# First image pair of a fused attention and spectral-convolution layer: transposes on the vector engine and through DRAM, long matmuls along h, inverse transforms with two row groups in two banks

## The chip, the cores and the metric

The kernel runs on one core of a Trainium2 chip. The metric is the device time of one execution in microseconds, the median over runs. A profile is one further execution, recorded instruction by instruction; "span" is the time from its first to its last instruction.

## The reference, cut to what matters

The input x has shape (4, 64, 96, 96): 4 images of 64 channels and 9216 pixels. Two residual layers follow each other.

```python
# layer 0: attention with a sigmoid over all pairs of pixels, channel gate
h = group_norm(x)                                   # 32 groups
Q, K, V = 1x1 convolutions of h (8, 8 and 64 channels), N = 96*96
att = sigmoid(einsum('bcn,bcm->bnm', Q, K))         # 9216 x 9216 per image
y = einsum('bcm,bnm->bcn', V, att) + h
gate = sigmoid(mlp(mean(y)) + mlp(max(y)))          # per channel
x = x + y * gate
# layer 1: spectral convolution
u = rfft2(group_norm(x), norm='ortho')
v = 0 except v[:, :, :16, :16] = einsum('bchw,cohw->bohw', u[:, :, :16, :16], R_pos)
             v[:, :, -16:, :16] = the same with u[:, :, -16:, :16] and R_neg
x = x + irfft2(v, norm='ortho')
```

Only 32 frequencies along h (KH) and 16 along w (KW) are kept, so the Fourier transforms are products with small constant matrices (fw, fh, gh, gw).

## The kernel before, in words

Two images share the 128 partitions (64 channels each): pair 0 and pair 1. Attention goes through 2 x 18 blocks of 512 query pixels. For one block there are 144 tiles of energies (72 chunks of 128 keys, 2 images), each one matmul (L441, on 32 rows, four row groups side by side) into one PSUM bank. ScalarE takes the sigmoid of several banks at once (L452) and writes `at`; TensorE multiplies `at` with the values (L470, 64 columns per image, two column groups side by side) and sums the block up in an accumulator bank.

The tiles of a block are handled in bursts of 6 or 7. `pattern` gives each block one list of burst sizes: `DENSE` (24 bursts of 6), `SPARSE` (21 bursts, nearly all of 7), `HALF` (22 bursts, 10 of 6 and 12 of 7). PSUM has 8 banks: one accumulates, a burst of 7 takes all the others, and a burst of 6 leaves one spare, `bank_a`. The loop at the end of the attention part writes down, for each burst number t: the energies of burst t + 1, then the steps of `mid[t]`, then the value matmuls of about one burst and the sigmoids of burst t + 1, then the steps of `end[t]`. TensorE follows this order.

The steps in `mid` are other work that uses the spare bank: keys, values and queries of later blocks, and, while pair 1 is in attention, the whole of layer 1 for pair 0 (class `Hidden`). `put(t, steps, every)` places each step at the next free t whose following burst has 6 tiles. VectorE and the DMA queue of SyncE (SP) get their instructions in an order that the framework's scheduler chooses within the dependencies; each is worked off strictly in order. A spare bank must be emptied by VectorE before the next burst of 7 can use it.

Layer 1 of pair 0 in steps (blocks 18 to 29):

- `result(s)`, 12 strips of 768 pixels: loads the input strip (`old`), adds the gated attention output in place on VectorE (`combine`, L162), takes statistics (L260); the strip is also stored to DRAM (`x1d`).
- `transposes(r)`, 24 steps: four TensorE transposes of 96 pixels x 128 channels (L270) into the spare bank, copied by VectorE to `xT` (L588).
- `along_w(m)`, 6 steps: four matmuls with fw (L280), each on 32 columns of the array, then a copy, and a way through DRAM (`ad`) that turns the layout into `ah` (rows h).
- statistics in 4 small steps (`st0` to `spread`), then `along_h(i)`, 4 steps: 32 matmuls each with `ah` as the stationary and 64 columns of fh as the moving operand (L307), scaled into `u` by VectorE (L313).
- `mix(q, half)`, 16 steps: products with the weights (L203), which SP streams in.
- `back_h(e, half, b)`, 8 steps: one matmul of 64 rows, 96 columns and 512 moving columns (L326), a copy, a way through DRAM (`zd`) to `z`.
- `back_w(i, x1d)`, 24 steps: two matmuls of 128 rows, 64 columns (one image each), 384 moving columns of gw, side by side (L348), added to the strip from `x1d` by VectorE (L351) and stored to the output.

`gw` is block diagonal: rows of one of its four 32-row blocks meet only the 96 output columns of one image row.

After attention, pair 1 does its own layer 1 in a tail of some 90 us that the change leaves alone (L716 to L831).

Of the kernel before, what the change touches and what calls it, by code (L numbers as in the profile page):

```python
# [40 lines left out]
P = 128  # L41
# [5 lines left out]
KW = 16  # L47
# [8 lines left out]
HALF = [6 if i == 1 or i % 2 == 0 and i < 18 else 7 for i in range(22)]  # L56
SPARSE = [6 if i in (0, 1, 11) else 7 for i in range(21)]
# [24 lines left out]
def tile_kernel(ctx: ExitStack, tc: tile.TileContext, x, cst, late, spec, out):  # L82
# [153 lines left out]
    class Hidden(Layer1):  # L236


        def __init__(self, p, gate, bank, move, work):
            super().__init__(p, gate, bank, move, (nc.sync,) * 3)  # L240
            self.work = work
            self.stats = small.tile([P, 2 * NSTRIP, 6], F32, tag="stats1", name=f"stats1_{p}")
            self.xts, self.ah = {}, None
            self.ad = dram.tile([H, 2 * KW, P], F32, tag=f"ad{p}", name=f"ad_{p}")
            self.zd = dram.tile([H, 2 * KW, 2, C], F32, tag=f"zd{p}", name=f"zd_{p}")
# [8 lines left out]
        def result(self, s):  # L254
            p, cols = self.p, bass.ts(s, STRIP)
            old = self.work.tile([P, STRIP], F32, tag="old", bufs=2, name=f"old_{p}_{s}")
            nc.sync.dma_start(old, xf[bass.ts(p, P), cols])
            self.combine(s, old)
            for i in (2 * s, 2 * s + 1):
                nc.vector.bn_stats(self.stats[:, i, :], xs[p][:, bass.ts(i, STRIP // 2)])  # L260
# [4 lines left out]

        def transposes(self, r):

            pt = self.bank(f"pt_{self.p}_{r}")
            for i in range(4):
                nc.tensor.transpose(pt[:W, bass.ts(i, P)], xs[self.p][:, bass.ts(4 * r + i, W)],  # L270
                                    ident)
            self.xts[r] = self.work.tile([W, NB], F32, tag="xT", bufs=4, name=f"xT_{self.p}_{r}")
            self.move(self.xts[r], pt[:W, :])

        def along_w(self, m):
# [3 lines left out]
            for g in range(4):  # L279
                nc.tensor.matmul(pa[bass.ts(g, 2 * KW), :], named("fw", W), self.xts[4 * m + g],  # L280
                                 start=True, stop=True)
# [12 lines left out]
        def along_h(self, i):  # L294

            b, half = i // 2, i % 2
            ah = self.ah.rearrange("h (s k b c) -> h s k b c", k=KW, b=2, c=C)
            u = self.ut[:, :U].rearrange("q (h k n s b) -> q n k s h b", h=KH, n=SIDE, s=2, b=2)
            if i == 0:
                nc.vector.memset(self.ut[:, U:], 0.0)  # L300
            pu = self.bank(f"pu_{self.p}_{i}")
            fh = named("fh", H)
            for k in range(KW // 2):
                for s in range(2):
                    for part in range(2):
                        first = KH * (2 - s - part)
                        nc.tensor.matmul(pu[bass.ts(part, C), bass.ts(k, 2 * KH)],  # L307
                                         ah[:H, s, half * (KW // 2) + k, b, :],
                                         fh[:, first:first + 2 * KH],
                                         start=(s == 0), stop=(s == 1))  # L310
            v = pu.rearrange("q (n k s h) -> q n k s h", n=2, s=2, h=KH)
            for n in range(2):
                nc.vector.tensor_scalar(u[:, 2 * half + n, :, :, :, b], v[:, n],  # L313
                                        self.rs[:, 0, b:b + 1], None, ALU.mult)
# [5 lines left out]
        def back_h(self, e, half, b):  # L320


            first = e * KW + half * (KW // 2)
            ks, rows = slice(first, first + KW // 2), bass.ts(b, 2 * KH)
            pz = self.bank(f"pz_{self.p}_{b}_{e}_{half}")
            nc.tensor.matmul(pz[:H, :], named("gh")[rows, bass.ts(e, H)],  # L326
                             self.vt[rows, bass.ts(half, KW // 2 * C)], start=True, stop=True)
            zt = self.work.tile([P, NB], F32, tag="ae", bufs=2, name=f"zt_{self.p}_{b}_{first}")
            self.move(zt[:H, :], pz[:H, :])
            nc.sync.dma_start(self.zd[:, ks, b, :],  # L330
                                     zt[:H, :].rearrange("h (k o) -> h k o", o=C))
            if b == 1:
                for j in range(4):
                    nc.sync.dma_start(
                        self.z[32 * j + first:32 * j + first + KW // 2, :, :],
                        self.zd[j::4, ks, :, :].rearrange("h k b o -> k h (b o)"))

        def back_w(self, i, x1d):

            s = i // 2  # L340
            cols = bass.ts(s, STRIP)
            if i % 2 == 0:
                self.old = self.work.tile([P, STRIP], F32, tag="old", bufs=2,
                                          name=f"x1_{self.p}_{s}")
                nc.sync.dma_start(self.old, x1d[:, cols])
            py = self.bank(f"py_{self.p}_{i}")
            for b in range(2):
                nc.tensor.matmul(py[bass.ts(b, C), :4 * W], self.z[:, i, bass.ts(b, C)],  # L348
                                 named("gw"), start=True, stop=True)
            o = self.old[:, bass.ts(i % 2, 4 * W)]  # L350
            nc.vector.tensor_tensor(o, py[:, :4 * W], o, ALU.add)  # L351
            if i % 2:
                nc.sync.dma_start(outf[bass.ts(self.p, P), cols], self.old)


    with tc.tile_pool(name="work", bufs=1) as work, \
# [11 lines left out]
        kT = kvp.tile([P, NCH // 2, P], F32R, tag="kT", name="kT")  # L368

# [64 lines left out]
        def bank_of(t):  # L434
            return 0 if sizes[t] == 7 and block[t] % 2 == 0 else 1
# [94 lines left out]
        pattern = [DENSE] + [SPARSE] * (NBLK - 2) + [DENSE] + [HALF] * 12  # L530
# [14 lines left out]
        def put(t, steps, every=1):  # L545
# [42 lines left out]
        l1 = Hidden(0, gate, bank_a, lambda dst, src: nc.vector.tensor_copy(dst, src), work)  # L588
        x1d = dram.tile([P, N], F32, tag="x1", name="x1d")
        for s in range(NSTRIP):  # L590
            end[first + 7 + 2 * s] += [lambda s=s: later(lambda: (
                l1.result(s), nc.sync.dma_start(x1d[:, bass.ts(s, STRIP)],
                                                xs[0][:, bass.ts(s, STRIP)])))]
        t = put(first + 9, [step for m in range(H // 16) for step in [
            lambda r=r: l1.transposes(r) for r in range(4 * m, 4 * m + 4)] + [
                lambda m=m: l1.along_w(m)]])
# [16 lines left out]
        t = put(t + 2, [lambda i=i: l1.along_h(i) for i in range(4)], 2)  # L613
# [9 lines left out]
        t = put(t + 5, [lambda i=i: l1.back_h(i // 4, i // 2 % 2, i % 2) for i in range(8)])  # L623
        t = put(t + 5, [lambda i=i: l1.back_w(i, x1d) for i in range(H // 4)])
# [293 lines left out]
```

## Time and profile before

| | us |
|---|---|
| runs | 3116.04, 3119.44, 3120.33 (median 3119.44) |
| profiled execution, its own time | 3118.38 |
| its span | 3116.6 |
| TensorE matmul busy | 3072.2 (99%) |
| ScalarE busy | 2424.6 (78%) |
| VectorE busy | 397.0 (13%) |
| mean granted TensorE clock | 0.995 |

1.8 us of the profiled execution lie outside its span. In the profile, a line such as L470 is a line of the kernel before; "x12" counts instructions; a float32 matmul shows as two matmul instructions (two passes). "out<-in" names tiles; "PEld" is TensorE's loading of the stationary operand. The tile `ws` is the memory of pair 0's x after it has been reused as workspace (`u`, weights, `z`), `room` is that of `ah` reused.

### The profile page before, as it was taken

To read this page: it belongs to the slowest core of one execution; us is meant where nothing else is said; L and a number is where in the kernel's file an instruction comes from. 1 tells how busy PE (TensorE), PEld (TensorE's weight loads), DVE (VectorE), ACT (ScalarE), POOL (GpSimd) and SP (SyncE) were. 2 spreads that over 40 slices of the span, in tenths; PEclk is the share of its full clock that TensorE was granted. 3 is DMA by queue.
4 is the path that set the end of the run, shared out by engine and by line. 5 is a ranking of instruction groups with operands and counts; after the bars stand their busy time and mean duration, and the time that the engine had idled before them with its cause. 6 is when DMAs were issued, how large, how long until landed. Compare 5 with 4: busy or idle time off the path is not lost.

```text
span 3116.6 us, 43034 instructions
## 1 busy us (share of the span) xinstructions
PE 3072.2 (99%) x19186; PEld 1147.4 (37%) x19186; DVE 397.0 (13%) x838; ACT 2424.6 (78%) x1585; POOL 24.5 (1%) x49
## 2 busy tenths in 40 slices
PE   6999999999999999999999999999999999999998
PEld 3433333333333333334433333333333333333335
DVE  5300000000000000002331110110101100000015
ACT  3788888888888888886777777777777788888871
POOL 0000000000000000000000000000000010000001
PEclk9999999999999999999999999999999999999998
DMA  3000000000000000000120010131210130000026
GB/s 143 1 1 1 1 1 1 1 1 1 1 1 1 1 1 1 1 1 1 41 88 14 8 36 13 52 125 44 36 34 31 41 120 1 1 1 1 6 74 216
DMA packets 39161, 88.87 MB, mean 29 GB/s; under 512 B 10336, under 2 KB 17248, under 8 KB 38880
## 3 DMA queue, kind: packets, MB, share of 16 engines
q1 hardware_dynamic: 31856, 61.88, 6.4%
q0 software_dynamic: 5344, 19.27, 1.7%
q10 hardware_dynamic: 1776, 4.97, 0.4%
q8 instruction: 150, 2.46, 0.3%
q14 instruction: 35, 0.29, 0.0%
HBM read 62.77 MB, written 23.33 MB: 28 GB/s over the span
## 4 chain that ended last, share of the span: by engine, by line
PE 97%; DVE 1%; DMA 1%; issue 0%; POOL 0%; SPq 0%; ACT 0%; POOLq 0%; DVEq 0%
PE banks L470 74%; PE banks L441 16%; PE banks L409 1%; PE banks L421 1%; PE banks L348 1%; PE banks L398 1%; PE banks L203 1%; DMA x<-in_x_dram 0%; PE py L825 0%; PE banks L270 0%; DVE x L162 0%; DMA old<-in_x_dram 0%; DMA vd<-vm 0%; DVE xt L724 0%; PE banks L326 0%
## 5 line engine op out<-in xcount | busy, mean ns | idle before, releaser
L452 ACT ACTIVATE at<-banks 128x1536 f32<-128x1536 f32 (+1 forms) x1548 | 2404.4, 1597 | 610.6 <-PE banks L441 546.8
L470 PE MATMUL banks<-at,vT 128*64 128x512 f32 (+1 forms) x11728 | 2395.2, 549 | 0.0
L470 PEld LDWEIGHTS banks<-at,vT 128*64 128x64 f32 x11728 | 780.4, 136 | 1348.9 <-issue 1294.1
L441 PE MATMUL banks<-q,kT 32*128 32x512 f32 x5184 | 571.4, 454 | 1.6 <-DVE xT L588 1.6
L441 PEld LDWEIGHTS banks<-q,kT 32*128 32x128 f32 x5184 | 232.9, 182 | 472.3 <-issue 301.5
L475 DVE SCALAR_TENSOR_TENSOR x<-banks,x 128x512 f32<-128x512 f32 x36 | 24.9, 692 | 897.7 <-PE banks L470 897.7
L378 DVE TENSOR_SCALAR full_q<-banks,cs 128x256 f32<-128x256 f32 x36 | 17.4, 484 | 858.8 <-PE banks L421 858.8
L409 PE MATMUL banks<-cs,x 128*64 128x128 f32 x576 | 41.6, 287 | 1.5 <-DVE full_k L378 0.6
L431 DVE CAST q<-q 32x256 fp32r<-32x256 f32 x144 | 40.9, 284 | 3.9
L351 DVE TENSOR_TENSOR x<-banks,x 128x384 f32<-128x384 f32 x24 | 13.4, 558 | 197.0 <-PE banks L348 156.9
L409 PEld LDWEIGHTS banks<-cs,x 128*64 128x64 f32 x576 | 32.3, 141 | 16.2 <-DVE full_k L378 14.6
L588 DVE COPY xT<-banks 96x512 f32<-96x512 f32 x24 | 16.5, 686 | 167.1 <-PE banks L270 167.1
L386 DVE SCALAR_TENSOR_TENSOR q<-high_q,cs,full_q 64x256 fp32r<-64x256 f32 x72 | 34.6, 480 | 2.4
L378 DVE TENSOR_SCALAR full_k<-banks,cs 128x256 f32<-128x256 f32 x36 | 17.4, 484 | 93.2 <-PE banks L398 93.2
L588 DVE COPY ws<-banks 128x512 f32<-128x512 f32 x16 | 11.1, 692 | 141.7 <-PE banks L203 141.7
L412 DVE TENSOR_TENSOR vT<-banks,cs 128x512 f32<-128x512 f32 x36 | 24.8, 689 | 8.4 <-PE banks L409 8.3
L398 PE MATMUL banks<-x,cs 128*64 128x256 f32 x144 | 24.2, 396 | 1.6 <-DVE x L149 1.5
L477 DVE TENSOR_REDUCE maxs<-x 128x1 f32<-128x512 f32 x36 | 24.7, 686 | 1.2
L421 PE MATMUL banks<-x,cs 128*64 128x256 f32 x144 | 23.9, 410 | 0.6 <-DVE full_k L378 0.6
L483 DVE BATCH_NORM_STATS2 stats<-x 128x6 f32<-128x512 f32 x36 | 22.1, 679 | 8.0 <-DMA x<-in_x_dram 8.0
L732 PE MATMUL pa<-xt,lc 128*128 128x256 f32 x72 | 18.9, 422 | 3.6 <-DVE xt L724 2.6
L725 ACT ACTIVATE vT<-x,less 128x768 f32<-128x768 f32 x12 | 11.2, 934 | 12.4 <-DVE x L162 8.4
(117 smaller groups left out, 452.2 us busy)
## 6 DMA issues: line engine op xcount, KB each, us to landing
ws<-in_spec_dram SPq DMA_DIRECT2D x20, 512.0 KB
x<-in_x_dram SPq DMA_DIRECT2D x15, 512.0 KB
out_dram<-x SPq DMA_DIRECT2D x18, 384.0 KB
room<-in_spec_dram SPq DMA_DIRECT2D x12, 512.0 KB
w<-in_spec_dram POOLq DMA_DIRECT2D x10, 512.0 KB, 6.9
old<-in_x_dram SPq DMA_DIRECT2D x12, 384.0 KB
x1d<-x SPq DMA_DIRECT2D x12, 384.0 KB
x<-x1d SPq DMA_DIRECT2D x12, 384.0 KB
```

The costliest lines, as they stand in the source:

```text
L203: self.last = nc.tensor.matmul(pv[bass.ts(g, 32), :].rearrange("q (n k o) -> q n k o", n=SIDE, o=C)[:, :, k, :], self.ut[:, at:at + 32], s ...
L348: nc.tensor.matmul(py[bass.ts(b, C), :4 * W], self.z[:, i, bass.ts(b, C)], named("gw"), start=True, stop=True)
L378: nc.vector.tensor_scalar(u, src, bias, None, ALU.add)
L386: mark[0] = nc.vector.scalar_tensor_tensor(dst, h.bitcast(F32), is_low, u, ALU.mult, ALU.add)
L398: nc.tensor.matmul(pp[cols, :NB // 2], named("wk")[:, cols], src[:, e, :, :], start=True, stop=True)
L409: nc.tensor.matmul(pp[bass.ts(e, P // 2), bass.ts(i, P)], xs[p][:, bass.ts(2 * (4 * s + i) + e, P // 2)], named("wv"), start=True, stop=True)
L421: nc.tensor.matmul(pq[rows, :half], named("wq")[:, rows], xs[p][:, n * NB + e * half:n * NB + (e + 1) * half], start=True, stop=True)
L431: nc.vector.tensor_copy(q[to:to + 32, cols], q[of:of + 32, cols])
L441: nc.tensor.matmul(banks[:, bank_of(t) + i - starts[t], :], kT[r:r + 32, i // 4, :], q[r:r + 32, :], start=True, stop=True)
L452: nc.scalar.activation(at[:, of + lo:of + hi, :], banks[:, bank + lo:bank + hi, :], AF.Sigmoid)
L470: nc.tensor.matmul(acc[half, cols], vT[:, j, half], at[:, place(2 * pair + b), cols], start=(j == 0), stop=(j == NCH - 1))
L588: l1 = Hidden(0, gate, bank_a, lambda dst, src: nc.vector.tensor_copy(dst, src), work)
```

## The change

It concerns layer 1 of pair 0 only, and the burst sizes of five blocks of pair 1.

- The 24 TensorE transpose steps are gone. `result` transposes the strip in 32 x 32 blocks on VectorE, writes it to DRAM (`xd`), and a new step `turned(s)` reads it back with three DMAs whose contiguous pieces are 32 elements (128 bytes). `xT` becomes 2 buffers of 1024 columns instead of 4 of 512. The load of `old` is issued one strip ahead (`fetch`). Strips are 6 bursts apart instead of 2, `along_w` steps at least 12.
- `along_h` has 2 steps instead of 4: fh (32 columns) is stationary, 512 columns of `ah` move, four column groups side by side, two rounds (s) that accumulate. VectorE transposes the result in 32 x 32 blocks and scales it with three instructions.
- `back_h` has 4 steps instead of 8: both images in one step, one on rows 0 to 63 and one on rows 64 to 127, into two banks; one copy of 1024 columns.
- `back_w` has 12 steps instead of 24: a strip at a time, four matmuls of 64 rows, 128 columns and 192 moving columns (the zero halves of gw are left out), row group k into bank k.
- Two spare banks need bursts of five: the pattern `PAIRS` (23 bursts: 7 of 5, 3 of 6, 13 of 7) is used for three blocks, `HALF` for seven instead of twelve, and two further blocks become `SPARSE`. `back_h` and `back_w` are put beside bursts of five only.

Burst numbers (the same count in both; pair 1 starts at 384): `along_w` at 407, 417, 433, 449, 459, 475 before and 407, 419, 431, 449, 455, 471 after; `along_h` at 493 to 499 before, 483 and 485 after; `mix` from 503 to 545 before, 493 to 529 after; `back_h` at 551 to 571 before, 540 to 549 after; `back_w` from 581 to 639 before, 563 to 598 after; the early loads of weights for the tail (`fetch`, on the POOL queue) at 670 before, 629 after. There are 774 bursts before and 775 after.

```diff
 HALF = [6 if i == 1 or i % 2 == 0 and i < 18 else 7 for i in range(22)]
+PAIRS = [5 if i % 3 == 0 and i else 6 if i in (0, 1, 11) else 7 for i in range(23)]
 SPARSE = [6 if i in (0, 1, 11) else 7 for i in range(21)]
...
-        def result(self, s):
-            p, cols = self.p, bass.ts(s, STRIP)
-            old = self.work.tile([P, STRIP], F32, tag="old", bufs=2, name=f"old_{p}_{s}")
-            nc.sync.dma_start(old, xf[bass.ts(p, P), cols])
+        def result(self, s, x1d):
+            cols, old = bass.ts(s, STRIP), self.olds[s]
+            if s + 1 < NSTRIP:
+                self.fetch(s + 1)
             self.combine(s, old)
+            nc.sync.dma_start(x1d[:, cols], xs[self.p][:, cols])
+            nc.vector.transpose(old, xs[self.p][:, cols])
+            nc.sync.dma_start(self.xd[s], old)
             for i in (2 * s, 2 * s + 1):
...
+        def turned(self, s):
+            self.xts[s] = self.work.tile([W, STRIP // W * P], F32, tag="xT", bufs=2,
+                                         name=f"xT_{self.p}_{s}")
+            for n in range(NSQ):
+                nc.sync.dma_start(
+                    self.xts[s][bass.ts(n, SQ), :].rearrange("w (h k c) -> w h k c", k=4, c=SQ),
+                    self.xd[s].rearrange("(k w) (h n c) -> n w h k c", k=4, n=NSQ, c=SQ)[n])
...
-        def transposes(self, r):
-            pt = self.bank(f"pt_{self.p}_{r}")
-            for i in range(4):
-                nc.tensor.transpose(pt[:W, bass.ts(i, P)], xs[self.p][:, bass.ts(4 * r + i, W)],
-                                    ident)
-            self.xts[r] = self.work.tile([W, NB], F32, tag="xT", bufs=4, name=f"xT_{self.p}_{r}")
-            self.move(self.xts[r], pt[:W, :])
...
-        def along_h(self, i):
+        def along_h(self, b):
...
+            for s in range(2):
+                for part in range(2):
+                    first = KH * (2 - s - part)
+                    for k in range(2):
+                        nc.tensor.matmul(pu[bass.ts(2 * part + k, SQ), :], fh[:, first:first + KH],
+                                         ah[:H, s, :, b, bass.ts(k, SQ)],
                                          start=(s == 0), stop=(s == 1))
+            t = self.work.tile([P, NB], F32, tag="ae", bufs=2, name=f"t_{self.p}_{b}")
+            nc.vector.transpose(t, pu)
...
-        def back_h(self, e, half, b):
+        def back_h(self, e, half):
...
+            pz = self.two_banks()
+            for b in range(2):
+                rows = bass.ts(b, 2 * KH)
+                nc.tensor.matmul(pz[:H, b, :], named("gh")[rows, bass.ts(e, H)],
+                                 self.vt[rows, bass.ts(half, KW // 2 * C)], start=True, stop=True)
+            zt = self.work.tile([H, 2, NB], F32, tag="xT", bufs=2, name=f"zt_{self.p}_{first}")
+            self.move(zt, pz[:H])
...
-        def back_w(self, i, x1d):
+        def back_w(self, s, x1d):
...
+            py = self.two_banks()
+            for i in range(2):
+                for k in range(2):
+                    rows = bass.ts(k, P // 2)
+                    nc.tensor.matmul(py[:, k, bass.ts(i, M)], self.z[rows, 2 * s + i, :],
+                                     named("gw")[rows, bass.ts(k, M)], start=True, stop=True)
...
+        def two_banks():
+            return banks[:, slice(0, 2) if spare[0] == 0 else slice(6, 8), :]
...
-            return 0 if sizes[t] == 7 and block[t] % 2 == 0 else 1
+            even = block[t] % 2 == 0
+            return {7: 0 if even else 1, 6: 1, 5: 2 if even else 1}[sizes[t]]
...
-        pattern = [DENSE] + [SPARSE] * (NBLK - 2) + [DENSE] + [HALF] * 12
+        pattern = [DENSE] + [SPARSE] * (NBLK - 2) + [DENSE] + [HALF] * 7 + [PAIRS] * 3
...
         for s in range(NSTRIP):
-            end[first + 7 + 2 * s] += [lambda s=s: later(lambda: (
-                l1.result(s), nc.sync.dma_start(x1d[:, bass.ts(s, STRIP)],
-                                                xs[0][:, bass.ts(s, STRIP)])))]
-        t = put(first + 9, [step for m in range(H // 16) for step in [
-            lambda r=r: l1.transposes(r) for r in range(4 * m, 4 * m + 4)] + [
-                lambda m=m: l1.along_w(m)]])
+            end[first + 7 + 6 * s] += [lambda s=s: later(lambda: l1.result(s, x1d))]
+            end[first + 9 + 6 * s] += [lambda s=s: l1.turned(s)]
+        for m in range(H // 16):
+            t = put(first + 22 + 12 * m, [lambda m=m: l1.along_w(m)])
```

## The prediction

> **What bounds the kernel now.** I read the page first, for who is busy and for the chain that ended last:
>
> ```profile
> PE 3072.2 (99%) x19186; PEld 1147.4 (37%) x19186; DVE 397.0 (13%) x838; ACT 2424.6 (78%) x1585; POOL 24.5 (1%) x49
> ...
> PE 97%; DVE 1%; DMA 1%; issue 0%; POOL 0%; SPq 0%; ACT 0%; POOLq 0%; DVEq 0%
> ```
>
> TensorE (PE) is the bound: 97% of the chain is its matmuls, ScalarE (ACT) has no share. But a busy PE says little about what one step is worth, so I went to the timeline of PE, where the start of one burst's energies (L441) to the next is the length of a burst:
>
> ```profile
> 1772.94 0.73 PE L441 MATMUL banks<-q,kT 32*128 32x512 f32 x6
> 1773.60 2.80 PE L470 MATMUL banks<-at,vT 128*64 128x512 f32 x12
> 1776.33 0.73 PE L441 MATMUL banks<-q,kT 32*128 32x512 f32 x6
> 1776.99 0.64 PE L270 MATMUL banks<-cs,x 128*96 128x128 f32 x4
> 1777.56 2.80 PE L470 MATMUL banks<-at,vT 128*64 128x512 f32 x12
> 1780.29 0.50 PE L441 MATMUL banks<-q,kT 32*128 32x512 f32 x4
> ```
>
> A bare burst of six takes 3.39 us, with a transpose step 3.96: the step lengthens it by all of its own time. Over the whole trace a bare burst of six has a median of 3.386, a bare one of seven 3.822, both constant to some 10 ns. So each step of `mid` costs what its burst has above 3.386. The same view at `along_h`, `back_h` and `back_w`:
>
> ```profile
> 1937.36 0.73 PE L441 MATMUL banks<-q,kT 32*128 32x512 f32 x6
> ...
> 1942.61 0.51 PE L441 MATMUL banks<-q,kT 32*128 32x512 f32 x4
> ```
>
> ```profile
> 2218.48 0.73 PE L441 MATMUL banks<-q,kT 32*128 32x512 f32 x6
> ...
> 2222.89 0.50 PE L441 MATMUL banks<-q,kT 32*128 32x512 f32 x4
> ```
>
> ```profile
> 2289.84 0.73 PE L441 MATMUL banks<-q,kT 32*128 32x512 f32 x6
> ...
> 2293.87 0.51 PE L441 MATMUL banks<-q,kT 32*128 32x512 f32 x4
> ```
>
> 5.25, 4.41 and 4.03 us. In excess of 3.386 (medians): transposes 0.574, `along_w` 0.996, `along_h` 1.867, `back_h` 1.027, `back_w` 0.646, half a `mix` 1.001, queries 0.436. Last, the one place where PE stood still in layer 1 of pair 0, PE's rows first, then VectorE's:
>
> ```profile
> 1615.19 0.73 PE L441 MATMUL banks<-q,kT 32*128 32x512 f32 x6
> 1617.52 0.49 PE L441 MATMUL banks<-q,kT 32*128 32x512 f32 x1 [1.59 <-DVE xT L588]
> ```
>
> ```profile
> 1615.85 1.02 DVE L162 SCALAR_TENSOR_TENSOR x<-x,gate,old 128x768 f32<-128x768 f32 x1 [4.98 <-DMA old<-in_x_dram]
> 1616.78 0.68 DVE L588 COPY xT<-banks 96x512 f32<-96x512 f32 x1
> ```
>
> The seventh energy waits for the spare bank, its copy is queued behind `combine`, and that waits for the strip loaded just before: this burst takes 5.91 instead of 3.82, 2.09 lost.
>
> **A unit for matmuls.** Value matmuls start a pass every 0.427 us for 512 columns, 0.833 ns a column; float32 needs two passes. `along_w`, 512 columns on four column groups at once, needs 0.853 and measures 0.996: 0.143 over. `back_h` is 0.174 over. Queries (two passes of 256 columns, 0.427) measure 0.436 and `back_w` (two of 384, 0.640) 0.646: next to nothing over. The difference: these two use the values' array shape, 128 x 64. The Trainium skill (TensorEngine Tiling (Array Packing), section Tiling Modes) says that changing the tiling mode drains TensorE. That speaks against this change: `back_w` leaves the values' shape for 64 x 128 and gets a drain that it did not have. I charge 0.17 for it; by the columns alone the result would be 2 us better.
>
> **The change part by part**
>
> *Transposes.* 24 x 0.574 = 13.8 us leave PE. What replaces them is off PE: on VectorE 12 transposes of 128x768 at 0.96 (the tail's L724 row: 958 ns) against 24 copies of 0.69 removed (L588), and VectorE is 13% busy; on SP 12 stores and 36 loads more. Cost nothing while the loads land before `along_w`; that is the first rival.
>
> *along_h.* Before 4 x 1.867 = 7.5. After: per step two rounds of four 512-column matmuls side by side, in `along_w`'s shape: 2 x 0.853 + 0.15 = 1.86, two steps 3.7. Gain 3.8. The moving pieces of 32 elements are no worry: the tail's L732 moves such pieces and keeps 0.216 a pass for 256 columns. VectorE's transpose (0.70 by L775) frees the bank in time.
>
> *back_h.* Before 8 x 1.027 = 8.2. After 4 steps with two row groups side by side. The tail shows that two 64-row groups overlap:
>
> ```profile
> L806 PE MATMUL pz<-vt,cs 64*96 64x256 f32 x32 | 6.0, 506 | 3.1 <-DMA vt<-vd 3.1
> L740 PE MATMUL pu<-a,lc 64*128 64x512 f32 x24 | 6.0, 615 | 0.6 <-DVE a L738 0.6
> ```
>
> 24 passes of 0.427 would be 10.2 us one by one; L740 was busy for 6.0. So a step is 1.04, four are 4.2, gain 4.1. If they ran one by one: 1.89 a step, 3.4 worse.
>
> *back_w.* Before 24 x 0.646 = 15.5. After, per step: 8 passes of 192 columns (0.16 each) in pairs, 0.64, plus 0.17: 0.81; twelve make 9.7, gain 5.8. Unknown: whether loading 128 weight columns hides behind only 0.16 us of moving. From below nothing is lost (L740 loads 128 columns behind 0.427; L806 loads 96 behind 256 columns at 0.216 a pair). From above the tail's L825 (32x128, 96 columns): 192 passes in threes took 14.4 us, 0.22 a round where 0.08 is needed, 0.14 exposed. With that a step is 1.4, 6.7 worse. I take 0.81: L806 is nearer in columns moved, and L825 picks its weights with a stride that `back_w` lacks.
>
> *Bursts.* Block lengths: `HALF` 10 x 3.386 + 12 x 3.822 = 79.72; `SPARSE` 78.95; a burst of five is one tile less than six, 3.386 - 0.436 = 2.95, so `PAIRS` 80.49. Five `HALF` fewer, three `PAIRS` and two `SPARSE` more: +0.8. Could ACT limit a burst of five? Its groups take 1.447 for three tiles and 1.02 for two (by the 1.878 for four), after 0.6 of energies: 3.06. 16 of the 21 bursts of five carry a step and are longer; the other five could cost 0.5 in all.
>
> *The stall.* The strip's load is now issued one strip ahead and six bursts lie between strips, so I count the 2.1 as gone; kept, it is 2.1 worse. What is late next: at the first `along_w` VectorE has the block's end (1.46), two `combine` (2.0), a transpose (0.96) and then the copy (0.69), 5.1 us, and the seventh energy needs the bank about 1.2 us later than that. The two-bank copies (1.25 us, by L738's 1.24 for 1024 columns; `back_w`'s add 0.96, between 0.56 for 384 and 1.36 for 1152) begin at most 1.7 us into bursts of 3.8 to 4.0. The `x1d` strips are loaded a step or more ahead, as before; a step every third burst leaves 11 us.
>
> *Queues.* SP's new loads stand behind stores that wait for VectorE, and `ad` and `ah` stand behind the loads; weights for `mix` keep their rhythm of before. POOL's early weight loads move 41 bursts forward, into a stretch where POOL has nothing else; the tail needs them much later.
>
> Sum: 13.8 + 3.8 + 4.1 + 5.8 + 2.1 - 0.8 = 28.8. Against the profiled execution (3118.4 with its 1.8 outside the span) 3089.6; it lies 1.1 below the median of the runs, so 3119.4 - 28.8 = 3090.6.
>
> **The rivals**
>
> *The transposed strips come late.* Two `xT` buffers mean that strips 8 and 9 can be loaded only after the fourth `along_w` (burst 449), and the fifth follows six bursts later: 4.38 + 3 x 3.39 + 2 x 3.82 - 1.0 = 21.2 us. In that window 6 DMAs of 1024 pieces of 128 B pass, 384 pieces per DMA engine, plus about 1.6 to start and land. The trace has no such piece. Nearest: `zd` stores, 768 pieces of 256 B in 1.30 us on 16 engines, 27 ns each; the strided `zd` read-back, 768 pieces of 512 B in 5.2 us on 8 engines, 54 ns each. 384 pieces take 10.4 to 20.7: no wait, or 1 us. I take 35 ns, no wait. At 80 ns PE waits 11 us there (3102). The skill speaks against this too: VectorE: DVE Perf Modes, section The three transpose paths, warns that a plain DMA copy that transposes by strides is 19 times slower than the DMA transpose. A packed strip passes in 8 packets of 121 ns per engine, 0.97 us; 19 times that is 18.4 per strip, 96 ns a piece. Then the fifth `along_w` waits 17, with the third and a late bank 5 more: 3113. I hold the warning for single elements; here each piece is 128 B. **Slower than before** begins at about 102 ns a piece, where the waits at the second, third and fifth `along_w` (2, 3 and 19.4) and the late bank (4) add up to 28.8; at 120 ns it would be 3140. (The fifth is 384 pieces + 1.6 - 21.2; the others come from laying the changed order of SP and VectorE on the durations above: the second and third have 44 us between them, of which two strips' loads and the stores and waits among them must pass.)
>
> *The row groups do not pay.* If weight loads are exposed (6.7) and the pairs do not overlap (3.4), 3101. For it: L825. Against it: L740, L806.
>
> *VectorE becomes late.* Each strip costs it 3.1 us in one piece (1.01 + 0.96 + 2 x 0.55), and one such stall cost 2.1 before; two new ones and the old one kept: 3097.
>
> *The gain isn't there,* because ACT paces the bursts: its two groups of a burst of six plus 0.6 also come to about 3.4. But a bare burst already runs at 3.386, so taking a step out reaches that in any case; I give it 2%.
>
> **How the numbers follow.** The sum as it stands 0.72; strips late by some us 0.10; late enough to be slower 0.03; row groups 0.08; VectorE 0.05; no gain 0.02. The likeliest time is 3090.6. Down, 5 us: no drain at `back_w` (2), cheaper switches, the scatter of the runs. Up: 3102 takes in exposed weight loads with overlap or strips late by 11, not the 19-fold case. So 3085.5 to 3102. A measurement of this kernel can tell about 0.2%, 6 us, from no change. Faster by more than that: everything but the slow end of the strips and the case without gain, 0.95; same 0.02; slower 0.03.
>
> **What would show it.** In the profile after: no L270 group; bursts of six at 3.39 where transposes stood; `along_h` steps 1.86 above 3.39; bursts of five of 2.95 bare, 3.99 with `back_h`, 3.76 with `back_w`; no wait of PE on `xd` loads or on a copy. Wrong: PE idle before an `along_w` on a DMA of `xT`; a burst with `back_w` near 4.4; a burst of seven above 3.9.

## The result, and the profile after

The changed kernel takes 3101.39 us (median of 4 runs, 3100.47 to 3102.19), the kernel before 3119.38 on the same chip: ratio 0.9944, interval 0.9927 to 0.9961. It gains 18.0 us where 28.8 were forecast; the time lies just inside the upper end of the range (3102). The profiled execution took 3100.47, its span is 3098.2.

In the profile after, the line numbers have moved: L466 are the energies, L477 the sigmoids, L495 the value matmuls, L292 `along_w`, L321 `along_h`, L347 `back_h`, L369 `back_w`, L615 the copies. The page, who is busy and the chain:

```profile
PE 3053.1 (99%) x18878; PEld 1135.4 (37%) x18878; DVE 388.6 (13%) x810; ACT 2421.6 (78%) x1587; POOL 24.5 (1%) x49
...
PE 96%; DVE 1%; DMA 1%; ACT 1%; issue 1%; POOL 0%; ACTq 0%; POOLq 0%; DVEq 0%
```

19 us of matmuls are gone and TensorE still carries the chain. One thing is new: ACT now has 1% of it, where it had none.

The steps, read as before from one burst's energies to the next. PE's timeline at `along_h`, then at a `back_h`, then at a `back_w`:

```profile
1884.99 0.73 PE L466 MATMUL banks<-q,kT 32*128 32x512 f32 x6
...
1890.23 0.73 PE L466 MATMUL banks<-q,kT 32*128 32x512 f32 x7
...
2113.04 0.73 PE L466 MATMUL banks<-q,kT 32*128 32x512 f32 x5
...
2117.03 0.74 PE L466 MATMUL banks<-q,kT 32*128 32x512 f32 x7
...
2202.37 0.73 PE L466 MATMUL banks<-q,kT 32*128 32x512 f32 x5
...
2206.17 0.73 PE L466 MATMUL banks<-q,kT 32*128 32x512 f32 x7
```

5.24, 3.99 and 3.80 us: `along_h` is 1.86 above a six, `back_h` 1.04 and `back_w` 0.85 above a bare five of 2.95. These are the lengths that the prediction named, `back_w` 0.04 above it. Where the strip held up the spare bank, PE's timeline at the first `along_w` now reads:

```profile
1601.58 0.73 PE L466 MATMUL banks<-q,kT 32*128 32x512 f32 x6
...
1605.96 0.73 PE L466 MATMUL banks<-q,kT 32*128 32x512 f32 x7
```

The seven energies at 1605.96 run through in 0.73: the 2.09 us stall is gone, and the burst before it is 4.38 long: a six and its step.

So the steps are as forecast, and 12 us are missing. They are found by laying the bare lengths (2.950, 3.386, 3.822) and the step costs on every burst. In blocks 18 to 24 nothing is over but the key, value and gate steps of block 18 and the small statistics steps, which the change leaves alone. In the three `PAIRS` blocks (25 to 27) and the one burst behind them 12.3 us are over, and nearly all of it lies on the bursts around a five: sevens that take 3.9 to 4.6 instead of 3.82. Two neighbouring fives with `back_h`, PE's timeline; the first is the one above (2113.04, followed by a seven at 2117.03; here its value matmuls), the second comes three bursts later:

```profile
2114.73 2.37 PE L495 MATMUL banks<-at,vT 128*64 128x256 f32 x12
...
2120.85 0.81 PE L466 MATMUL banks<-q,kT 32*128 32x512 f32 x7
...
2124.75 0.73 PE L466 MATMUL banks<-q,kT 32*128 32x512 f32 x5
2125.41 1.10 PE L347 MATMUL banks<-room,cs 64*96 64x512 f32 x4
2126.45 2.37 PE L495 MATMUL banks<-at,vT 128*64 128x512 f32 x12
2128.74 1.10 PE L466 MATMUL banks<-q,kT 32*128 32x512 f32 x7
2129.78 3.23 PE L495 MATMUL banks<-at,vT 128*64 128x256 f32 x16
2132.93 0.50 PE L466 MATMUL banks<-q,kT 32*128 32x512 f32 x4
2133.79 0.50 PE L466 MATMUL banks<-q,kT 32*128 32x512 f32 x3 [0.35 <-ACT at L477]
...
2137.38 0.73 PE L466 MATMUL banks<-q,kT 32*128 32x512 f32 x5
```

After the first five the sevens take 3.82 and 3.90; after the second 4.19 (2128.74 to 2132.93) and 4.45 (to 2137.38), and PE waits for ACT. ACT's timeline of the same stretch, with what each group of sigmoids waited for:

```profile
2115.49 1.45 ACT L477 ACTIVATE at<-banks 128x1536 f32<-128x1536 f32 x1 [0.82 <-PE banks L495]
...
2121.47 3.22 ACT L477 ACTIVATE at<-banks 128x2048 f32<-128x2048 f32 x2 [0.36 <-PE banks L466]
2125.35 1.02 ACT L477 ACTIVATE at<-banks 128x1024 f32<-128x1024 f32 x1 [0.66 <-PE banks L466]
2127.61 1.45 ACT L477 ACTIVATE at<-banks 128x1536 f32<-128x1536 f32 x1 [1.24 <-PE banks L495]
2130.52 6.33 ACT L477 ACTIVATE at<-banks 128x2048 f32<-128x2048 f32 x4 [1.45 <-PE banks L495]
```

Here is the reading. Two bare sevens in ACT's timeline before:

```profile
1757.70 3.22 ACT L452 ACTIVATE at<-banks 128x2048 f32<-128x2048 f32 x2 [0.60 <-PE banks L441]
1761.53 3.22 ACT L452 ACTIVATE at<-banks 128x2048 f32<-128x2048 f32 x2 [0.61 <-PE banks L441]
```

A bare seven needs 0.6 us of energies and 3.22 us of sigmoids: 3.82, its whole length. ACT, busy 78% of the span, has no slack in a burst of seven. At the second five it waits 1.24 us and then 1.45 us for *value matmuls* (L495), does four groups without a pause (6.33), and the energies of the following sevens find their banks still full.

Why it waits is in the addressing of `at`. It has 14 slots; bursts alternate between slots 0 to 6 and 7 to 13, each burst at the end of its half. A sigmoid group of burst t + 1 writes where burst t - 1 lies, so the values of burst t - 1 must have been read. The order of the work keeps the values 8 tiles behind the energies: when burst t has 7 tiles, 1 tile of burst t - 1 is still unread; when burst t has 5, 3 tiles are. From this:

1. The five's own second group waits for the last tile of the burst before the last, whose value matmuls come first among the five's. Values take tiles in pairs (a chunk for both images), and where their count comes out odd only half the query columns of the last pair. So these first matmuls (a row shows the shape of its first) have 512 columns if the five begins at an even tile of its block, 256 if at an odd one. The second five is even: its group starts 1.16 us after them (2126.45, 2127.61) and ends at 2129.06, after the next energies have begun (2128.74). The first is odd: 0.76 after them (2114.73, 2115.49), ended at 2116.94, before the next energies (2117.03). The step beside the five makes the wait long (1.24) but moves values and next energies alike; `bare_pairs` below has fives without a step.
2. The seven after the five finds 3 tiles unread, in slots 4 to 6. Its second group (slots 4 to 6) waits for them. If the five begins at an even tile, the values have also left half of slot 3 unread, and the *first* group (slots 0 to 3) waits too (the 1.45).

I call this theory A. Theory B: VectorE's copies of two banks hold up the first energies of the next seven. Where an expectation names a further reading, it says there what that is.

### The profile page after: what moved, and what is told of

It is laid out like the page before. It is cut to its first block, busy times and chain, and to the rows that moved or that the text cites. A ratio compares the mean times of both kernels' runs of the same rounds, so it can differ in the third digit from the quotient of the medians.

```text
span 3098.2 us, 42466 instructions
## 1 busy us (share of the span) xinstructions
PE 3053.1 (99%) x18878; PEld 1135.4 (37%) x18878; DVE 388.6 (13%) x810; ACT 2421.6 (78%) x1587; POOL 24.5 (1%) x49
## 4 chain that ended last, share of the span: by engine, by line
PE 96%; DVE 1%; DMA 1%; ACT 1%; issue 1%; POOL 0%; ACTq 0%; POOLq 0%; DVEq 0%
PE banks L495 75%; PE banks L466 17%; PE banks L433 1%; ACT at L477 1%; PE banks L445 1%; PE banks L422 1%; PE banks L204 1%; DMA x<-in_x_dram 0%; PE py L852 0%; PE banks L369 0%; DVE x L163 0%; DVE xt L751 0%; DMA vd<-vm 0%; PE banks L292 0%; PE pv L204 0%
## 5 line engine op out<-in xcount | busy, mean ns | idle before, releaser
L477 ACT ACTIVATE at<-banks 128x1536 f32<-128x1536 f32 (+2 forms) x1550 | 2401.4, 1596 | 597.8 <-PE banks L466 523.3
L495 PE MATMUL banks<-at,vT 128*64 128x512 f32 (+1 forms) x11740 | 2397.4, 549 | 0.0
L495 PEld LDWEIGHTS banks<-at,vT 128*64 128x64 f32 x11740 | 779.2, 136 | 1351.0 <-issue 1295.8
L466 PE MATMUL banks<-q,kT 32*128 32x512 f32 x5184 | 579.9, 455 | 3.4 <-ACT at L477 3.3
L466 PEld LDWEIGHTS banks<-q,kT 32*128 32x128 f32 x5184 | 236.5, 182 | 480.6 <-issue 327.9
L615 DVE COPY ws<-banks 128x512 f32<-128x512 f32 x16 | 11.1, 692 | 134.6 <-PE banks L204 114.3
L372 DVE TENSOR_TENSOR x<-banks,x 128x768 f32<-128x768 f32 x12 | 11.5, 958 | 101.7 <-ACT at L477 101.7
L752 ACT ACTIVATE vT<-x,less 128x768 f32<-128x768 f32 x12 | 11.2, 933 | 12.4 <-DVE x L163 8.4
L133 PE MATMUL banks<-mv_l,cs 128*128 128x1 f32 x6 | 1.4, 295 | 19.8 <-DVE mv_l L129 19.8
```

What stands on the lines that cost most here:

```text
L466: nc.tensor.matmul(banks[:, bank_of(t) + i - starts[t], :], kT[r:r + 32, i // 4, :], q[r:r + 32, :], start=True, stop=True)
L477: nc.scalar.activation(at[:, of + lo:of + hi, :], banks[:, bank + lo:bank + hi, :], AF.Sigmoid)
L495: nc.tensor.matmul(acc[half, cols], vT[:, j, half], at[:, place(2 * pair + b), cols], start=(j == 0), stop=(j == NCH - 1))
```

## The experiments

The measured loss of a run is the sum, over its three `PAIRS` blocks and the burst behind them, of what each burst has above its bare length and its step (1.04 for `back_h`, 0.81 for `back_w`, 0.44 for queries); for the changed kernel 12.3 us. Of these 8.1 lie on the two bursts behind each of the nine fives entered even, 2.2 on the sevens behind the three fives that follow a six, 0.6 is `back_w` itself (0.856, not 0.81), and the rest comes in pieces of 0.05 to 0.15. Where an expectation says 11.6 or 11.7 it leaves out the burst behind; where it counts about ten or eleven even fives there are nine, and twelve odd.

**Only the places of the fives.** Same numbers of fives, sixes and sevens, in another order. First all fives entered at an odd tile (alt_odd), then all at an even one (alt_even):

```diff
-PAIRS = [5 if i % 3 == 0 and i else 6 if i in (0, 1, 11) else 7 for i in range(23)]
+PAIRS = [6, 6, 7, 5, 7, 5, 7, 5, 7, 5, 7, 6, 5, 7, 5, 7, 5, 7, 7, 7, 7, 7, 7]    # alt_odd
+PAIRS = [6, 6, 5, 7, 5, 7, 5, 7, 5, 7, 5, 6, 7, 5, 7, 5, 7, 7, 7, 7, 7, 7, 7]    # alt_even
```

> The changed kernel with the order of the bursts inside a PAIRS block changed: 6 6 7 5 7 5 7 5 7 5 7 6 5 7 5 7 5 7 and five more of 7. Counts and sizes stay (7 of 5, 3 of 6, 13 of 7), and so do the steps beside the bursts of five. Every five now begins after an odd number of tiles of its block. Theory A (the ring of 14 at slots: when a five begins after an even number of tiles, the value matmuls behind it leave a pair of tiles half read in the fourth slot that the first sigmoid group of the next seven has to write; ScalarE, which has no slack in bursts of seven, falls behind and TensorE waits): the 11.7 us lost in bursts of seven in the three blocks shrink to about 3, time 3092 to 3094. Theory B (the copy of two banks holds up the next burst's energies): nothing changes, 3101, the sevens behind a step stay long. Theory C (a burst of five costs the next bursts time whatever its place): 3101 or longer, since each five has fewer sevens to recover in.

> As the run before, but every five begins after an even number of tiles: 6 6 5 7 5 7 5 7 5 7 5 6 7 5 7 5 and seven more of 7. Theory A: every five now loses about 1.0 us in the sevens behind it (in the changed kernel about half of them do), 21 us in place of 11.7: 3109 to 3112. Theories B and C: the same time as the run with odd places, about 3101.

alt_odd: 3094.27 us, ratio 0.9926 (0.9911 to 0.9941), loss 5.3. alt_even: 3109.47, ratio 0.997 (0.9959 to 0.9981), loss 19.8. The same work in the same mix, 15 us apart by the parity of the tile at which a five begins. Theory B, and the theory C of the expectation (each five costs the same wherever it stands), asked for about 3101 both times. alt_odd kept somewhat more loss than expected (5.3, not 3): the seven behind a five that follows a six still takes up to 4.62. There the five's second group finds 2 tiles unread, not 1; odd2 below takes that place away. The row of the waits view that moves with the parity (us in total, times, longest), in alt_even:

```profile
ACT at L477 <- PE banks L495: 98.0, 101, 1.8
```

and in the changed kernel:

```profile
ACT at L477 <- PE banks L495: 72.6, 95, 1.7
```

In alt_odd it is 59.0.

**The third part undone** (no_third): transposes and `along_h` new, `back_h`, `back_w` and twelve `HALF` blocks as before.

```diff
-        pattern = [DENSE] + [SPARSE] * (NBLK - 2) + [DENSE] + [HALF] * 7 + [PAIRS] * 3
+        pattern = [DENSE] + [SPARSE] * (NBLK - 2) + [DENSE] + [HALF] * 12
...
-        t = put(t + 5, [lambda i=i: l1.back_h(i // 2, i % 2) for i in range(4)], free=free_pairs)
-        t = put(t + 12, [lambda s=s: l1.back_w(s, x1d) for s in range(NSTRIP)], free=free_pairs)
+        t = put(t + 5, [lambda i=i: l1.back_h(i // 4, i // 2 % 2, i % 2) for i in range(8)])
+        t = put(t + 5, [lambda i=i: l1.back_w(i, x1d) for i in range(H // 4)])
```

> The changed kernel with its third part undone: back_h and back_w and the twelve HALF blocks as before, so no burst of five; the transposes on the vector engine and the long matmuls along h stay. If the whole shortfall is in the bursts around the fives: 13.8 (transposes) + 3.8 (along h) + 2.1 (stall) below the kernel before, 3099.7, a little faster than the whole change. If the shortfall comes from the first part (the 36 loads with pieces of 128 bytes, more work on VectorE): 3106 to 3111.

3099.07 us (3098.21 to 3101.27), ratio 0.9941 (0.9926 to 0.9956). The first two parts bring their 19.7 by the prediction's terms (13.8 + 3.8 + 2.1) and measure 18.9. The third part, worth 9.1 by its terms, brought nothing in the order in which it was written.

**The fives alone** (bare_pairs): the kernel before, with `PAIRS` in three blocks (31 to 33) where layer 1 has no steps left. Nothing is copied out of two banks here.

```diff
+PAIRS = [5 if i % 3 == 0 and i else 6 if i in (0, 1, 11) else 7 for i in range(23)]
...
-            return 0 if sizes[t] == 7 and block[t] % 2 == 0 else 1
+            even = block[t] % 2 == 0
+            return {7: 0 if even else 1, 6: 1, 5: 2 if even else 1}[sizes[t]]
...
+        pattern += [SPARSE, PAIRS, PAIRS, PAIRS]
```

> The kernel before with three late SPARSE blocks (31 to 33) turned into PAIRS blocks, without any step beside the fives. By the bare lengths of the prediction 3 x (80.5 - 78.95) = 4.6 slower, 3124.0. Theory A: the sevens behind bare fives are long as well, about 4 a block more, 3134 to 3137. Theory B (copies of two banks): 3124, since nothing is copied.

3134.95 us, ratio 1.0058 (1.0043 to 1.0073): 17.0 slower. By bare lengths three `PAIRS` for three `SPARSE` cost 3 x 1.54 = 4.6; the other 12.4 (12.6 by its trace) is the loss of the changed kernel, with no step of layer 1 and no copy of two banks near. Theory B falls. Nor does the loss need a step beside the five. In its waits view (L454 are the sigmoids, L472 the values, L443 the energies) the row below was 62.6 before; then a bare five entered even, PE's timeline and ACT's:

```profile
ACT at L454 <- PE banks L472: 82.7, 135, 1.8
```

```profile
2646.85 0.73 PE L443 MATMUL banks<-q,kT 32*128 32x512 f32 x5
2647.51 2.37 PE L472 MATMUL banks<-at,vT 128*64 128x512 f32 x12
2649.81 1.10 PE L443 MATMUL banks<-q,kT 32*128 32x512 f32 x7
...
2654.00 0.50 PE L443 MATMUL banks<-q,kT 32*128 32x512 f32 x4
...
2658.44 0.73 PE L443 MATMUL banks<-q,kT 32*128 32x512 f32 x5
```

```profile
2648.68 1.45 ACT L454 ACTIVATE at<-banks 128x1536 f32<-128x1536 f32 x1 [0.21 <-PE banks L472]
```

The five's second group waits only 0.21, yet it starts 1.17 after the values and ends at 2650.13, again 0.32 after the next energies have begun, and the sevens behind take 4.19 and 4.44, with the step 4.19 and 4.45.

**Slot 3 out of the first group.** In a seven after a five the groups become three and four tiles instead of four and three: in the changed kernel (split_after) and in alt_even (alt_even_split).

```diff
-            for lo, hi in ((0, size - 3), (size - 3, size)):
+            cut = 3 if size == 7 and t and sizes[t - 1] == 5 else size - 3
+            for lo, hi in ((0, cut), (cut, size)):
```

> The changed kernel, but in each burst of seven that follows a burst of five the sigmoid groups are three and four tiles (slots 0 to 2 and 3 to 6) instead of four and three. Theory A (the first group of that seven waits because its fourth tile, slot 3, is still being read by the value matmuls of a five that was entered with an even number of tiles): with slot 3 in the second group the first need not wait, about 0.63 us less at each of the ten or so fives entered even; the loss of 11.6 us in the three PAIRS blocks falls to 5 to 6, 3101.4 becomes 3095 to 3097. If instead it is only the second group of the five (held behind the back step) that costs the time: unchanged within 1.5 us, 3100 to 3103.

> alt_even (every five entered with an even number of tiles, 3109.5) with the same swap of the sigmoid groups in the seven after a five. Theory A: about 20 fives times 0.6 us come back, 3109.5 becomes 3096 to 3099. If the first group's fourth slot is not what is waited for: 3108 to 3111.

alt_even_split: 3099.94 us, ratio 0.9942 (0.9929 to 0.9954), loss 10.7: 9.5 us came back, a little less than expected. split_after: 3102.12, ratio 0.9944 (0.9932 to 0.9957), loss 12.9: nothing. That expectation was wrong. The next pair of runs shows what it had left out.

**All fives odd, and none right after the six** (odd2), **and the same with the swapped groups** (odd2_split).

```diff
-PAIRS = [5 if i % 3 == 0 and i else 6 if i in (0, 1, 11) else 7 for i in range(23)]
+PAIRS = [6, 6, 7, 5, 7, 5, 7, 5, 7, 5, 7, 6, 7, 7, 5, 7, 5, 7, 5, 7, 7, 7, 7]
```

> PAIRS = [6,6,7,5,7,5,7,5,7,5,7,6,7,7,5,7,5,7,5,7,7,7,7]: every five entered with an odd number of tiles, and none directly after the six. Theory A: alt_odd (3094.3) still lost some 0.8 us per PAIRS block at the bare five behind the six, 5.2 us in all; here 2.4 to 3.5 us are left: 3091 to 3093.5. Without effect of that place: 3094 to 3095.

> odd2 with the swapped sigmoid groups in the seven after a five. Theory A: no five is entered even, so slot 3 is free when the seven starts and the swap brings nothing: within 1.5 us of odd2, 3090 to 3094. If the swap of groups helps for another reason (a shorter first group lets the values start sooner everywhere) it gains as much here as in split_after, 5 us or more under odd2.

odd2: 3092.85 us (3091.55 to 3093.43), ratio 0.9917 (0.9903 to 0.993), loss 3.1. This is the fastest version, 8.5 us under the changed kernel (7.3 by what each gains on the kernel before beside it), with every instruction of it and another list of 23 numbers. PE's timeline, then ACT's:

```profile
2118.55 0.74 PE L466 MATMUL banks<-q,kT 32*128 32x512 f32 x7
...
2122.38 0.81 PE L466 MATMUL banks<-q,kT 32*128 32x512 f32 x5
...
2126.44 0.74 PE L466 MATMUL banks<-q,kT 32*128 32x512 f32 x7
```

```profile
2119.17 3.47 ACT L477 ACTIVATE at<-banks 128x2048 f32<-128x2048 f32 x2 [0.70 <-PE banks L466]
2122.98 1.02 ACT L477 ACTIVATE at<-banks 128x1024 f32<-128x1024 f32 x1 [0.34 <-PE banks L466]
2124.90 1.45 ACT L477 ACTIVATE at<-banks 128x1536 f32<-128x1536 f32 x1 [0.90 <-PE banks L495]
```

The seven takes 3.83, the five with `back_h` 4.06; the first group of the seven waits for its energies alone (0.70), and the two groups take 3.47 together, 0.25 more than in a bare seven.

odd2_split: 3101.16 us, ratio 0.9944 (0.9931 to 0.9958), loss 11.5: 8.3 slower than odd2, against both readings that had been written down. The same place, PE and then ACT:

```profile
2119.76 0.50 PE L466 MATMUL banks<-q,kT 32*128 32x512 f32 x3
2120.50 0.50 PE L466 MATMUL banks<-q,kT 32*128 32x512 f32 x2 [0.24 <-ACT at L478]
```

```profile
2116.51 1.45 ACT L478 ACTIVATE at<-banks 128x1536 f32<-128x1536 f32 x1 [0.66 <-PE banks L466]
2118.57 2.82 ACT L478 ACTIVATE at<-banks 128x2048 f32<-128x2048 f32 x2 [0.61 <-PE banks L496]
```

The short first group ends early; the second, now slots 3 to 6, waits 0.61 for the old values in slots 4 to 6, as the second group always had to. But it is four tiles long, 1.88 instead of 1.45, and ends 0.43 later: the following five grows from 4.06 to 4.51. So in split_after the swap saved about 0.5 at each five entered even and cost 0.43 at each entered odd; nine of the one and twelve of the other nearly cancel.

**The swap at even fives only** (split_even).

```diff
-            for lo, hi in ((0, size - 3), (size - 3, size)):
+            even = size == 7 and t and sizes[t - 1] == 5 and starts[t - 1] % 2 == 0
+            cut = 3 if even else size - 3
+            for lo, hi in ((0, cut), (cut, size)):
```

> The changed kernel, with groups of three and four tiles in the seven after a five only where that five was entered with an even number of tiles of its block. The swap in split_after took 0.5 us off at these and put 0.43 us on at the others (there the second group waits for the values of an earlier seven, and being four tiles long it ends 0.43 later). Theory A, so mended: only the saving is left; about eleven fives entered even times 0.4 to 0.5: 3101.4 becomes 3096 to 3098. If the two effects cannot be parted by the parity: 3100 to 3103.

3096.46 us (3095.47 to 3098.93), ratio 0.993 (0.9917 to 0.9944), loss 8.2: 4.9 under the changed kernel (4.0 by the gains), as expected. ACT's timeline where the 1.45 stood (L479 are the sigmoids, L497 the values), then PE's:

```profile
2127.80 1.45 ACT L479 ACTIVATE at<-banks 128x1536 f32<-128x1536 f32 x1 [1.24 <-PE banks L497]
2129.83 1.45 ACT L479 ACTIVATE at<-banks 128x1536 f32<-128x1536 f32 x1 [0.58 <-PE banks L466]
2131.52 1.88 ACT L479 ACTIVATE at<-banks 128x2048 f32<-128x2048 f32 x1 [0.23 <-PE banks L497]
```

```profile
2128.93 1.10 PE L466 MATMUL banks<-q,kT 32*128 32x512 f32 x7
...
2133.12 0.83 PE L466 MATMUL banks<-q,kT 32*128 32x512 f32 x7
...
2137.04 0.73 PE L466 MATMUL banks<-q,kT 32*128 32x512 f32 x5
```

The first group no longer waits for values; the second seven takes 3.92 instead of 4.45. The first still takes 4.19: that is point 1, the five's own second group, which the swap does not touch.

**The step behind the old values** (even_late): alt_even_split, with the step beside a five issued after the value matmuls that the five's second group waits for, in blocks 25 and 27. Its `PAIRS` and its swap are those of alt_even_split; the rest of its edit is

```diff
-            for step in mid[t]:
+            held = t + 1 < T and sizes[t + 1] == 5 and block[t + 1] % 2 == 1
+            for step in [] if held else mid[t]:
                 step()
...
             attend(items[:old])
+            for step in mid[t] if held else []:
+                step()
```

> alt_even_split (3099.9), with the back step beside a five put behind the old value matmuls for which the second sigmoid group of the five waits, in blocks 25 and 27 (in block 26 the spare banks are the first ones that the next seven needs). Theory A: the second group of the five ends about 1 us earlier, so the 0.37 us at the seven after it, and the 0.1 to 0.16 at the five, go for the eight or nine steps in these blocks: 4 us, less 0.15 for each further change of the array's shape: 3095 to 3098. If the second group does not wait because of the step's place: 3099 to 3102.

3099.82 us (3099.32 to 3102.64), ratio 0.9942 (0.9929 to 0.9954): no different from alt_even_split, so the expected 3095 to 3098 was missed. The trace shows the half that came true, PE first, then ACT (L478 sigmoids, L496 values):

```profile
2118.63 0.83 PE L466 MATMUL banks<-q,kT 32*128 32x512 f32 x5
...
2122.87 0.73 PE L466 MATMUL banks<-q,kT 32*128 32x512 f32 x7
...
2126.69 0.83 PE L466 MATMUL banks<-q,kT 32*128 32x512 f32 x5
```

```profile
2120.55 1.45 ACT L478 ACTIVATE at<-banks 128x1536 f32<-128x1536 f32 x1 [0.30 <-PE banks L496]
2123.44 1.45 ACT L478 ACTIVATE at<-banks 128x1536 f32<-128x1536 f32 x1 [1.44 <-PE banks L466]
```

The five's second group waits 0.30 instead of 1.3, and the seven after it is back at 3.82 from 4.19: with the step between the first values and the next energies the group has the time that it lacked, as point 1 says. (The step in its old place was not the cause: the 0.37 is there at bare fives too.) But the five grew from 4.10 to 4.24, where the values are now split around the step. Five and seven together gain 0.23, not 0.4; over the eight such pairs (a ninth five, followed by a six, gains nothing) the loss falls by 1.7 (10.7 to 8.9), and the medians, which scatter by more, do not show it.

The runs in one table. What is left when the loss read from the trace of one execution is taken off the median time moves by 2.6 us, where the times differ by 16.6. In the traces the time before block 18 differs by 2.7 us from run to run, and that from block 35 on by 4.5, so the 2.6 need no further cause:

| | time, us | loss in the three blocks | time less loss |
|---|---|---|---|
| changed kernel | 3101.39 | 12.3 | 3089.1 |
| alt_odd | 3094.27 | 5.3 | 3089.0 |
| alt_even | 3109.47 | 19.8 | 3089.6 |
| split_after | 3102.12 | 12.9 | 3089.3 |
| alt_even_split | 3099.94 | 10.7 | 3089.3 |
| odd2 | 3092.85 | 3.1 | 3089.8 |
| odd2_split | 3101.16 | 11.5 | 3089.6 |
| split_even | 3096.46 | 8.2 | 3088.3 |
| even_late | 3099.82 | 8.9 | 3090.9 |

## Why the prediction was right, and where its sum was wrong

Direction and range held; the likeliest time was 10.8 us too low. That the range held is partly luck: its upper edge, 3102, stood for exposed weight loads or late strips, and neither came. The same bursts in another order (alt_even, 3109.5) would have fallen outside. By its own terms, from the traces:

| term | forecast | measured |
|---|---|---|
| transposes | 13.8 | 13.8: bursts of six are bare, and PE waits for no transposed strip |
| `along_h` | 3.8 | 3.8 (2 x 1.857 for 4 x 1.867) |
| `back_h` | 4.1 | 4.1 (4 x 1.040) |
| `back_w` | 5.8 | 5.2 (12 x 0.856, not 0.81) |
| stall | 2.1 | 2.1 |
| bursts | -0.8 | -12.5 |
| sum | 28.8 | 16.5 |

From the start of block 18 to the start of block 35 the trace is 16.6 us shorter. The rest of the profiled difference (18.4 in the span) is 0.9 longer before that stretch and 2.7 shorter behind it; both are within what these stretches differ by from run to run. Five of the six terms hold, so the failed step is one: **Bursts**, mis-sized by 11.7. It took the block lengths from bare bursts, which had been measured with sixes and sevens alone, and asked "Could ACT limit a burst of five?" only for the work inside the five (1.447 + 1.02 + 0.6 = 3.06). Two things were missing: where ACT writes, and that a delay is paid in the burst behind, a seven, in which ACT has no slack. Both could be had from the trace of before and the code: 3.22 + 0.6 = 3.82 is a bare seven's whole length, and `place` and `done` say how much is still unread. The sign that it named for itself, "a burst of seven above 3.9", is what the trace shows. With the bursts in the order of odd2 the same instructions gain 25.3 of the 28.8 forecast.

*The transposed strips come late:* they do not. The waits of PE list no `xT` load. What the 128-byte pieces took can now be seen, first in the queue's row of the two pages (packets, MB, share of 16 engines), before and after:

```profile
q1 hardware_dynamic: 31856, 61.88, 6.4%
```

```profile
q1 hardware_dynamic: 71024, 71.32, 8.1%
```

39168 packets more took 8.1% x 16 x 3098.2 - 6.4% x 16 x 3116.6 = 824 us more of engine time. 36864 of them are these pieces; 1536 are the rows of 3072 bytes of the new stores to `xd`. The packet records of the trace part the two: 570 us for the pieces, 15.5 ns each, and 192 us for the stores. In the window that the prediction feared, behind the fourth `along_w`, the 6144 pieces passed in 6.35 us on 16 engines, 16.5 ns each. I had taken 35; the waits would have begun near 51 ((21.2 - 1.6) / 384). The warning in the Trainium skill (VectorE: DVE Perf Modes, The three transpose paths), as the prediction turned it into an estimate, would have made it 96 ns. The page speaks of a large innermost stride at the destination and compares with the hardware DMA transpose, which no run here uses; for these pieces, contiguous over 128 bytes, the estimate does not hold.

*The row groups do not pay:* they do. That rival's number, 3101, is the measured time, but its cause is not there: `back_h` is 1.04 and `back_w` 0.856, so pairs overlap, and (see the drain, next) weights load behind 192 columns. A time that fits does not make a cause.

*The drain at `back_w`:* the trace sides with the Trainium skill (TensorEngine Tiling (Array Packing), Tiling Modes), by which a change of tiling mode drains TensorE. In the values' shape the step had 0.006 above its columns, in 64 x 128 it has 0.216 (0.856 - 0.640); 0.17 was charged. Weight loads that stick out would lengthen each of its four rounds. But by the starts of its matmuls the rounds in the middle follow after 0.16, their columns alone; the first takes 0.27 and the last, up to the values, 0.26. So nearly all of the 0.216 lies at the two changes of shape; what TensorE does there no run shows. "By the columns alone 2 us better" is refuted.

*VectorE becomes late:* PE's waits list none on a copy (L615). *The gain isn't there because ACT paces the bursts:* dismissed since a bare six runs at 3.386. For sixes that was right. The rival had the right engine, in the wrong burst.

## What to carry to other kernels

When a change puts a new kind of step into a pipelined loop, price it with its neighbours: write down for the engine with the least slack what each of its instructions must wait for, its output slots too, one and two rounds later. An engine at 78% busy can have no slack at all in the rounds that matter. Where a ring is reused and the consumer lags by a fixed count, changing the round's size changes how much is still unread; try the order of the sizes before the work itself, since here a list of 23 numbers moved the time from 3092.9 to 3109.5. And a remedy that helps one kind of round is tried on the other kind too: the swap of groups was worth 0.5 us at one parity and cost 0.43 at the other.

## What the runs showed of the hardware that was not expected

- A strided read-back in pieces of 128 bytes cost 15.5 ns a piece on a DMA engine, and 36 such loads (4.7 MB) hid entirely behind attention: PE waited for none of them.
- Loading 128 weight columns for 192 moving columns on two row groups stayed hidden between rounds (0.16 us from round to round, the columns' own time); 0.216 us for the whole step of 8 passes were over, about half where the array's shape changes and half where it changes back.
- Splitting the value matmuls once more around a step cost about 0.15 us at each place (even_late: the five grew from 4.10 to 4.24).
